# Where the projections' side work stands: stores a product later, pieces of x from the keys on, unpacking from the eighth product on

## The chip, the cores and the metric

The kernel runs on one core of a Trainium2 chip. The metric is the device time of one execution in microseconds (us), as the median of the runs; less is better. The engines are TensorE (PE), VectorE (DVE), ScalarE (ACT), GpSimd (POOL) and SyncE (SP), which here only issues DMAs. Each engine takes its instructions in the order of its own list.

## The reference, cut to what matters

One layer on x of 2 batches x 1024 tokens x 1024 columns. Both branches read the same layer norm.

```python
xn = _layernorm(x, axis=-1)
# attention: 32 heads of 32, 8 key/value heads, rotary angles on q and k, causal
q, k, v = xn @ wq, xn @ wk, xn @ wv          # 1024, 256 and 256 columns
s = softmax(mask(rope(q) @ rope(k).T / sqrt(32))) @ v @ wo
# feed-forward with 4-bit weights, 2 x 2752 columns inside
w_gu = scale[g_idx] * (nibble(qweight) - (nibble(qzeros) + 1)[g_idx])
gate, up = split(xn @ w_gu)
g = silu((silu(gate) * up) @ w_d)            # w_d is unpacked likewise
return x + s * g
```

## The kernel before

**Stages.** For each of the two batches the kernel makes the layer norm, turned so that the 1024 columns lie on partitions (`xnT`), then runs `project`, `attend` and `project_out`. The feed-forward of both batches comes last. `project` of batch 0 lies at about 27 to 258 us of the profile, that of batch 1 at about 700 to 912 us.

**Seven products for eight.** `project` multiplies `xnT` with five pairs of weight tiles, each tile 128 columns wide: pair 0 holds the first two tiles of the keys' weights, pairs 1 to 4 the queries'. (Keys have 256 columns, so one pair covers them.) A pair is done as a 2x2 block product in Strassen's manner: tokens, contraction and columns are halved, and sums of blocks (`sums` for x, `quarters` for weights) let seven products stand for eight. A product is four matmuls of 128x512 (eight PE instructions, 3.44 us at full clock, line L455). The generator `pair` yields after each, in the order 1, 5, 2, 6, 3, 7, 4. The loop over pairs interleaves two of these generators, so that product 4 of a pair comes after product 1 of the next: the variable `slot` numbers all products from 1 to 35, and slots 1 to 8 are products 1, 5, 2, 6, 3, 7 of the keys, 1 of the first pair of queries and 4 of the keys. After them `values(t)` makes the values `v` for eight blocks of 128 tokens (L503), with two buffers `ps_v` in PSUM that ACT copies out (L506).

**What a product sets off.** `sum_of` adds a product to an earlier sum (`u`, `p`: L466, L484, DVE); `turn_heads` applies the rotary angles (L417 and L419 on DVE, L420 and L421 on POOL) and puts a function `leave` on the list `leaving`. `leave` splits the rotated tile in a high part (`rot_hi`, ACT, L425) and the rest (`rot_lo`, DVE, L427), and issues both stores to DRAM on SP (L428, L429).

**Side work, in `others`.** `project` runs under `manual_schedule`: every engine gets its instructions in the order in which the program writes them. After each product `others(n)` is called:

```python
while len(leaving) > n:
    leaving.pop(0)()
if splits and slot % 2:
    splits.pop(0)()
next(side, None)
```

First come the splits of rotated tiles. Then, at odd slots, comes one piece of x (`split_x`): `x_hi` on ACT (L511), `x_lo` on DVE (L513) and two stores of 256 KB to `xs_dram` on SP (L514, L515); the feed-forward reads them later. There are 16 pieces in a batch, and four are put on the list with each pair from pair 1 on, so the first lies at slot 11, and the last two at slots 37 and 39, among the values. Last comes one step of `side`. In batch 0 that is `look`, which surveys the scales, zeros and group indices (L141 to L208 on DVE), reduces a flag to one number (`one`, L232, then a matmul at L234), and issues from ACT eight spreading loads `zb_gu` (L240) and 21 of `zb_d` (L245). In batch 1 it is `unpack` for eight units of 256 weight columns, 35 steps: SP loads `qw` and `zt` (L256, L258), DVE takes the nibbles (`nib`, L272 to L277), ACT makes floats (`nf`, L281), POOL issues the store to `ng` (L263).

**Loads and maxima.** In the loop over pairs, ahead of a pair's third product, SP is given the loads of the turned keys (`head.keys`, pair 1, L631), then of the values' weights (L370) and of the next pair's weights `w_qk` (L364); at pair 2 the 16 loads of turned queries (`head.queries`, L636). From there on `head.rows` makes the row maxima of the first head group's scores a step at a time between matmuls and among the values: products `s` on PE (L671, L677), maxima `mx` on DVE (L687), and `mrow` (L724). Two score buffers tie PE to the maxima.

**Pools.** `rot_hi`, `rot_lo`, `x_hi`, `x_lo`, `qw`, `zt` and `nib` have two buffers each.

Of the kernel before, what the change touches and what calls it, by code (L numbers as in the profile page):

```python
# [10 lines left out]
F32 = mybir.dt.float32  # L11
F32R = mybir.dt.float32r
# [6 lines left out]
ALU = mybir.AluOpType  # L19
# [4 lines left out]
P = 128  # L24
# [12 lines left out]
def block_kernel(  # L37
# [18 lines left out]
    nc = tc.nc  # L56
# [9 lines left out]
    NC = D // P  # L66
    KH = NS
    TB = 512
    NB = T // TB
# [44 lines left out]
    xs_dram = [dram.tile([2, P, NS, T], F32, name=f"xs_{b}", tag=f"xs_{b}") for b in range(B)]  # L114
# [251 lines left out]
    def load_kv(pool, w_dram, w=None):  # L366

        if w is None:
            w = pool.tile([P, NS, N_KV * HD], F32, name="w_kv")
        nc.sync.dma_start(w, w_dram.rearrange("(g p) n -> p g n", p=P))  # L370
        return w

    def project(b, xnT, w_k, qs, ks, v, side, head, S, places):
# [5 lines left out]
        with tc.tile_pool(name="qkv_w", bufs=1, reuse_waits="tile") as wp, tc.tile_pool(name="qkv", bufs=2, reuse_waits="tile") as pool, tc.tile_pool(  # L379
            name="qkv_t", bufs=1, reuse_waits="tile"  # L380
        ) as tp, tc.tile_pool(name="qkv_ps", bufs=3, space=PSUM, reuse_waits="tile") as psp, tc.tile_pool(
            name="v_ps", bufs=2, space=PSUM, reuse_waits="tile"
# [16 lines left out]
            def quarters(wa, wb):  # L399


                low, high = slice(0, H), slice(H, NS)
                t = [wp.tile([P, H, P], F32, name=f"t_{i}") for i in range(2)]
                nc.vector.tensor_tensor(t[0], wb[:, low], wa[:, low], ALU.subtract)
                nc.vector.tensor_tensor(t[1], wb[:, high], t[0], ALU.subtract)
                nc.gpsimd.tensor_tensor(wb[:, low], wb[:, high], wb[:, low], ALU.subtract)
                B = {1: wa[:, low], 2: wa[:, high], 3: wb[:, high], 5: t[0], 6: t[1], 7: wb[:, low]}
                yield B
                B[4] = wp.tile([P, H, P], F32, name="t_2")
                nc.gpsimd.tensor_tensor(B[4], wa[:, high], t[1], ALU.subtract)  # L410
                yield B

            def turn_heads(c, n, dst):

                tok = slice(n * TB, (n + 1) * TB)
                t1 = pool.tile([P, TB], F32, name="rot1")
                nc.vector.tensor_tensor(t1, c, cs[:, 0, tok], ALU.mult)  # L417
                t2 = pool.tile([P, TB], F32, name="rot2")
                nc.vector.stream_shuffle(t2, c, swap)  # L419
                nc.gpsimd.tensor_tensor(t2, t2, cs[:, 1, tok], ALU.mult)  # L420
                nc.gpsimd.tensor_tensor(t1, t1, t2, ALU.add)  # L421

                def leave():
                    hi = pool.tile([P, TB], F32R, name="rot_hi")
                    nc.scalar.copy(hi, t1)  # L425
                    lo = pool.tile([P, TB], F32R, name="rot_lo")
                    nc.vector.tensor_tensor(lo, t1, hi.bitcast(F32), ALU.subtract)  # L427
                    nc.sync.dma_start(dst[0, :, tok], hi.bitcast(F32))  # L428
                    nc.sync.dma_start(dst[1, :, tok], lo.bitcast(F32))  # L429

                leaving.append(leave)

            leaving, splits = [], []
            slot = 0

            def others(n=1):


                while len(leaving) > n:
                    leaving.pop(0)()  # L440
                if splits and slot % 2:
                    splits.pop(0)()
                next(side, None)

            def pair(B, dsts):

# [23 lines left out]
                product(1, A[0, 0], 0, True)  # L470
                nc.scalar.copy(p1, banks[0])
                others()
                yield
                product(5, S[0], 2, True)
                nc.scalar.copy(p5, banks[2])
                nc.gpsimd.tensor_tensor(p5, p1, p5, ALU.add)
                others(0)
                yield
                product(2, A[0, 1], 0, False)
                turn_heads(banks[0], 0, dsts[0])  # L480
                others()
                yield
                product(6, S[1], 1, True)
# [21 lines left out]
                    )  # L505
                nc.scalar.copy(v[:, t, :], ps)  # L506

            def split_x(c, n):
                tok = slice(n * TB, (n + 1) * TB)
                hi = xp.tile([P, TB], F32R, name="x_hi")  # L510
                nc.scalar.copy(hi, xnT[:, c, tok])  # L511
                lo = xp.tile([P, TB], F32R, name="x_lo")
                nc.vector.tensor_tensor(lo, xnT[:, c, tok], hi.bitcast(F32), ALU.subtract)  # L513
                nc.sync.dma_start(xs_dram[b][0, :, c, tok], hi.bitcast(F32))  # L514
                nc.sync.dma_start(xs_dram[b][1, :, c, tok], lo.bitcast(F32))  # L515

            def weights(i):
                return [load_w(places, wq, c, tag=f"room_{1 + NREP + c % 4}") for c in (2 * i - 2, 2 * i - 1)]  # L520
# [10 lines left out]
            for i in range(PAIRS):  # L531
                dsts = (ks[0], ks[1]) if i == 0 else (qs[2 * i - 2], qs[2 * i - 1])
                g = pair(B, dsts)
                next(g)
                for _ in running or ():
                    next(make)
                next(g)

                if i == 1:
                    head.keys()  # L540
                    w = load_kv(None, wv, w_k)
                if i == 2:
                    head.queries()
                if 0 < i < PAIRS - 1:
                    loads.append(weights(i + 1))
                if i:
                    splits += [lambda c=c, n=n: split_x(c, n) for c in (2 * i - 2, 2 * i - 1) for n in range(NB)]
                for _ in range(3):
                    next(g)
                if i == 2:  # L550

                    work = head.rows()
                if i + 1 < PAIRS:
                    make = quarters(*loads[i + 1])
                    B = next(make)
                next(g)
                running = g
            next(running)
            others(0)

            warm = tp.tile([P, 1], F32, name="warm")
            nc.scalar.activation(warm, eps, AF.Exp)
# [996 lines left out]
    def open_x():  # L1559
        st = ExitStack()  # L1560
        xp = st.enter_context(tc.tile_pool(name="x", bufs=1, side="right", reuse_waits="tile"))
        return st, xp.tile([P, NS, T], F32, name="xnT"), xp

    ffn_open = ExitStack()
    x_open, xnT, xp = open_x()
# [4 lines left out]
    for b in range(B):  # L1570
# [5 lines left out]
        with tc.tile_pool(name="at_first", bufs=1, reuse_waits="tile") as fp, tc.tile_pool(  # L1576
            name="qkv_T", bufs=1, reuse_waits="tile"
        ) as qp:

            room = [q0p.tile([P, T], F32R, name=f"room_{j}") for j in range(1 + NREP)]  # L1580
            v = qp.tile([P, NT, N_KV * HD], F32, name="v")
            with tc.tile_pool(name="ps_s", bufs=1, space=PSUM, reuse_waits="tile") as ps_s:
                head = Maxima(qs_dram[b], ks_dram[b], fp, ps_s, room)
                if b == 0:
                    with tc.tile_pool(name="prep", bufs=1) as pool, tc.tile_pool(
                        name="prep_ps", bufs=1, space=PSUM
                    ) as psp:
                        first = look(pool, psp)
                        project(b, xnT, w_k, qs_dram[b], ks_dram[b], v, first, head, oT, q0p)
                        for _ in first:  # L1590
                            pass
                else:
                    with tc.tile_pool(name="unpack", bufs=2, side="right", reuse_waits="tile") as up:
                        side = unpack(up, range(11, 19), False)
                        project(b, xnT, w_k, qs_dram[b], ks_dram[b], v, side, head, oT, q0p)
                        for _ in side:
                            pass
                x_open.close()

                room += [q0p.tile([P, T], F32R, name=f"room_{j}") for j in range(1 + NREP, 1 + 2 * NREP)]  # L1600
                output = Output(b, oT, q0p)
                attend(head, v, oT, output)
        if b == B - 1:
            ffn_args = start_ffn(ffn_open)
            xnT = xp = None
        else:
            x_open, xnT, xp = open_x()
        with tc.tile_pool(name="unpack", bufs=3, side="right", reuse_waits="tile") as up:
            side = unpack(up, range(11) if b == 0 else range(19, NF), b == B - 1)
# [62 lines left out]
```

## Time and profile before

| | |
|---|---|
| runs | 2365.11, 2359.92, 2359.94 us |
| median | 2359.94 us |
| profiled execution | 2352.96 us, span 2351.1 us, mean granted clock 0.983 |
| PE, DVE, ACT, POOL busy | 2222.8, 1528.2, 1142.2, 854.1 us |
| `project` of batch 0, about 231 us (27 to 258) | PE busy 180.09 us, DVE 140.28, ACT 32.10, POOL 80.13 |

The span runs from the first to the last instruction; 1.86 us of the profiled execution lie around it. A row of a timeline gives the start, the length, the engine (with q for its queue of DMA issues), the line, the operation, the tile written and the tiles read, a shape, a count, and in brackets the idle time ahead of it with what ended it. A row of waits gives who waited for whom, the total in us, how often, and the longest. A row of the table by stretch gives its ends and length, the busy time of PE, of PE's weight loads, of DVE, ACT and POOL with their instruction counts, then the granted clock of PE, the mean busy share of the DMA engines, and GB/s.

### The profile page before, as it was taken

To read this page: it belongs to the slowest core of one execution; us is meant where nothing else is said; L and a number is where in the kernel's file an instruction comes from. 1 tells how busy PE (TensorE), PEld (TensorE's weight loads), DVE (VectorE), ACT (ScalarE), POOL (GpSimd) and SP (SyncE) were. 2 spreads that over 40 slices of the span, in tenths; PEclk is the share of its full clock that TensorE was granted. 3 is DMA by queue.
4 is the path that set the end of the run, shared out by engine and by line. 5 is a ranking of instruction groups with operands and counts; after the bars stand their busy time and mean duration, and the time that the engine had idled before them with its cause. 6 is when DMAs were issued, how large, how long until landed. Compare 5 with 4: busy or idle time off the path is not lost.

```text
span 2351.1 us, 30837 instructions
## 1 busy us (share of the span) xinstructions
PE 2222.8 (95%) x11233; PEld 1530.0 (65%) x11233; DVE 1528.2 (65%) x2336; ACT 1142.2 (49%) x1838; POOL 854.1 (36%) x599
## 2 busy tenths in 40 slices
PE   7894999999998879999999999999999999999997
PEld 4343655554883446555547878888878888878875
DVE  7773477774436774777751366776778677777875
ACT  2111345544242223544451466555778655556875
POOL 3550376776035552777771200000135200000362
PEclk9997999999998999999999999999999999999999
DMA  5645131311476864322216923232555655332475
GB/s 156 212 156 189 39 88 46 82 46 31 158 229 209 250 206 104 88 49 60 67 34 230 314 69 81 57 78 81 222 173 196 197 139 144 94 81 94 131 232 154
DMA packets 262185, 309.52 MB, mean 132 GB/s; under 512 B 19147, under 2 KB 197707, under 8 KB 261880
## 3 DMA queue, kind: packets, MB, share of 16 engines
q1 hardware_dynamic: 245172, 260.62, 37.3%
q0 software_dynamic: 10752, 38.02, 5.3%
q10 hardware_dynamic: 6100, 8.82, 1.2%
q8 instruction: 91, 1.49, 0.3%
q14 instruction: 70, 0.57, 0.1%
HBM read 214.58 MB, written 97.03 MB: 133 GB/s over the span
## 4 chain that ended last, share of the span: by engine, by line
PE 73%; POOL 7%; DMA 6%; issue 6%; DVE 5%; ACT 2%; SPq 1%; ACTq 1%; POOLq 0%; DVEq 0%
PE acc L1321 27%; PE acc L1202 11%; PE st L784 7%; PE s L677 7%; PE o L831 5%; PE ps_wo L1003 5%; PE l L849 3%; PE ps_v L503 2%; PE st L799 2%; PE ps L455 2%; DMA w_qk<-in_L_attn_wq 1%; POOL rot L420 1%; PE s L671 1%; POOL rot L421 1%; POOL p L944 1%
## 5 line engine op out<-in xcount | busy, mean ns | idle before, releaser
L1321 PE MATMUL acc<-x,w 128*128 128x512 f32 x2752 | 640.3, 393 | 2.3 <-ACT acc L1089 1.3
L1321 PEld LDWEIGHTS acc<-x,w 128*128 128x128 f32 x2752 | 512.4, 188 | 121.7 <-DVE h L1294 7.4
L1091 DVE TENSOR_SCALAR acc<-acc,r_gu 128x1024 f32<-128x1024 f32 x301 | 389.1, 1293 | 166.0 <-PE acc L1321 162.5
L687 DVE TENSOR_REDUCE mx<-s 128x1 f32<-128x512 f32 (+3 forms) x672 | 383.9, 608 | 173.0 <-PE s L671 88.0
L809 ACT ACTIVATE p<-st 128x512 f32<-128x512 f32 (+3 forms) x768 | 314.7, 496 | 314.6 <-PE st L799 313.3
L1089 ACT ACTIVATE acc<-acc,r_gu 128x1024 f32<-128x1024 f32 x301 | 327.4, 1088 | 232.3 <-PE acc L1321 228.7
L1305 POOL TENSOR_TENSOR h_lo<-h,h_hi 128x512 fp32r<-128x512 f32 x78 | 100.3, 1287 | 805.4 <-PE acc L1202 588.9
L944 POOL TENSOR_TENSOR p<-p 128x2048 f32<-128x2048 f32 (+3 forms) x122 | 359.9, 2954 | 9.3 <-PE o L831 4.9
L1091 DVE TENSOR_SCALAR acc<-acc,r_d 128x512 f32<-128x512 f32 x320 | 241.6, 759 | 62.3 <-PE acc L1202 60.0
L1089 ACT ACTIVATE acc<-acc,r_d 128x512 f32<-128x512 f32 x320 | 210.9, 663 | 61.8 <-PE acc L1202 55.1
L1003 PE MATMUL ps_wo<-oT,w_o 128*128 128x256 f32 x1024 | 232.1, 382 | 0.0
L1202 PE MATMUL acc<-h_lo,w 128*128 128x512 f32 (+1 forms) x576 | 228.9, 397 | 2.9 <-POOL h_lo L1305 2.6
L1202 PE MATMUL acc<-h_hi,w 128*128 128x512 f32 (+1 forms) x576 | 229.5, 399 | 0.7 <-ACT h_hi L1304 0.7
L1003 PEld LDWEIGHTS ps_wo<-oT,w_o 128*128 128x128 f32 x1024 | 191.1, 190 | 40.9 <-issue 16.7
L812 POOL TENSOR_SCALAR_AFFINE_SELECT p<-p 128x512 f32<-128x512 f32 x128 | 80.3, 634 | 242.2 <-ACT p L809 242.2
L831 PE MATMUL o<-p,v 128*32 128x512 f32 (+3 forms) x1536 | 162.9, 496 | 0.9 <-POOL p L812 0.9
L677 PE MATMUL s<-kst,room 128*128 128x512 f32 (+3 forms) x384 | 130.5, 379 | 0.0
L1202 PEld LDWEIGHTS acc<-h_lo,w 128*128 128x128 f32 (+1 forms) x576 | 108.4, 188 | 30.7 <-POOL h_lo L1305 5.1
L1202 PEld LDWEIGHTS acc<-h_hi,w 128*128 128x128 f32 (+1 forms) x576 | 108.3, 188 | 30.6 <-issue 3.0
L784 PE MATMUL st<-room,kst 128*128 128x512 f32 (+3 forms) x384 | 119.1, 371 | 3.2 <-ACT p L809 3.2
L281 ACT ACTIVATE nf<-nib 128x1024 fp32r<-128x1024 uint8 (+2 forms) x68 | 67.7, 1039 | 90.5 <-DVE nib L277 40.0
L677 PE MATMUL s<-room,room 128*128 128x512 f32 (+3 forms) x96 | 52.9, 578 | 61.5 <-DVE mx L687 46.4
(193 smaller groups left out, 2705.1 us busy)
## 6 DMA issues: line engine op xcount, KB each, us to landing
w<-ng SPq DMA_DIRECT2D x86, 512.0 KB
w<-nd SPq DMA_DIRECT2D x63, 512.0 KB
ng<-nf POOLq DMA_DIRECT2D x42, 512.0 KB, 7.6
room<-qs SPq DMA_DIRECT2D x160, 128.0 KB
x<-xs SPq DMA_DIRECT2D x32, 512.0 KB
qst<-qs SPq DMA_DIRECT2D x96, 128.0 KB
xt<-in_L_attn_x SPq DMA_DIRECT2D x16, 512.0 KB
w_qk<-in_L_attn_wq SPq DMA_DIRECT2D x16, 512.0 KB
```

Of the source, the lines that this page charges most:

```text
L677: nc.tensor.matmul(s[:, c * w : (c + 1) * w], q[j][:, qt * P : (qt + 1) * P], k[:, k0:k1], start=n == 1, stop=c == n - 1 and (n > 1 or not ...
L687: nc.vector.tensor_reduce(mx[:, at, js[0] : js[0] + n, k0 // TB], s[:, : w * n].rearrange("p (j t) -> p j t", j=n), AX.X, ALU.max)
L784: nc.tensor.matmul(s[:, q0:], kst[g][:, kt * P : (kt + 1) * P], stack[g][j][:, qlo + q0 : qlo + TB], start=True, stop=False,)
L809: nc.scalar.activation(p[:, j, q0:], st[j][:, q0:], AF.Exp, scale=1.0 / math.sqrt(HD))
L831: nc.tensor.matmul(o[HD * j : HD * (j + 1), q0:], v[:, kt, HD * g : HD * (g + 1)], p[:, j, q0:], start=(kt == 0), stop=last,)
L944: what(*args)
L1003: self.last = nc.tensor.matmul(ps[:, c * self.BLK : (c + 1) * self.BLK], self.ws[c0 + c][:, g, :], self.oT[:, g, t0 : t0 + self.BLK], star ...
L1089: nc.scalar.mul(a, a, r)
L1091: nc.vector.tensor_scalar(a, a, r, None, ALU.mult)
L1202: nc.tensor.matmul(acc[c], w[:k, c * P : (c + 1) * P], ht[:k, :], start=(f == 0 and t == 0), stop=(t == 1), skip_group_check=(f > 0),)
L1305: nc.gpsimd.tensor_tensor(at[1][:k, :], h[:k, f, tok], at[0][:k, :].bitcast(F32), ALU.subtract)
L1321: nc.tensor.matmul(a[:, n, :], w[i][:, g * P : (g + 1) * P], xs[t][:, g, n * TB : (n + 1) * TB], start=(g == 0 and t == 0), stop=(t == 1), ...
```

## The change

Three things are altered in `project`. Stores of `rot_hi`, `rot_lo`, `x_hi` and `x_lo` are put on a list `going`, and `send` issues them at the start of the next `others`, and also ahead of `head.keys` and `head.queries`. A piece of x is made at every even slot from 2 on, so that the 16 are made at slots 2 to 32. In batch 1 `side` takes no step at slots 1 to 7; its 35 steps begin at slot 8, and the last of them come among the values. In batch 0 `side` is stepped as before.

```diff
                     lo = pool.tile([P, TB], F32R, name="rot_lo")
                     nc.vector.tensor_tensor(lo, t1, hi.bitcast(F32), ALU.subtract)
-                    nc.sync.dma_start(dst[0, :, tok], hi.bitcast(F32))
-                    nc.sync.dma_start(dst[1, :, tok], lo.bitcast(F32))
+                    going.append((dst[0, :, tok], hi))
+                    going.append((dst[1, :, tok], lo))
 
                 leaving.append(leave)
 
-            leaving, splits = [], []
+            def send():
+
+                for to, what in going:
+                    nc.sync.dma_start(to, what.bitcast(F32))
+                going.clear()
+
+            leaving, going = [], []
             slot = 0
 
             def others(n=1):
 
 
+                send()
                 while len(leaving) > n:
                     leaving.pop(0)()
-                if splits and slot % 2:
-                    splits.pop(0)()
-                next(side, None)
+                if slot % 2 == 0:
+                    next(splits, None)
+                if b == 0 or slot > 7:
+                    next(side, None)
...
-            def split_x(c, n):
-                tok = slice(n * TB, (n + 1) * TB)
-                hi = xp.tile([P, TB], F32R, name="x_hi")
-                nc.scalar.copy(hi, xnT[:, c, tok])
-                lo = xp.tile([P, TB], F32R, name="x_lo")
-                nc.vector.tensor_tensor(lo, xnT[:, c, tok], hi.bitcast(F32), ALU.subtract)
-                nc.sync.dma_start(xs_dram[b][0, :, c, tok], hi.bitcast(F32))
-                nc.sync.dma_start(xs_dram[b][1, :, c, tok], lo.bitcast(F32))
+            def split_x():
+                for c in range(NC):
+                    for n in range(NB):
+                        tok = slice(n * TB, (n + 1) * TB)
+                        hi = xp.tile([P, TB], F32R, name="x_hi")
+                        nc.scalar.copy(hi, xnT[:, c, tok])
+                        lo = xp.tile([P, TB], F32R, name="x_lo")
+                        nc.vector.tensor_tensor(lo, xnT[:, c, tok], hi.bitcast(F32), ALU.subtract)
+                        going.append((xs_dram[b][0, :, c, tok], hi))
+                        going.append((xs_dram[b][1, :, c, tok], lo))
+                        yield
+
+            splits = split_x()
...
+                send()
                 if i == 1:
                     head.keys()
                     w = load_kv(None, wv, w_k)
                 if i == 2:
                     head.queries()
                 if 0 < i < PAIRS - 1:
                     loads.append(weights(i + 1))
-                if i:
-                    splits += [lambda c=c, n=n: split_x(c, n) for c in (2 * i - 2, 2 * i - 1) for n in range(NB)]
...
             next(running)
             others(0)
+            send()
+            for _ in splits:
+                send()
```

## The prediction

> **What bounds the kernel now.** I read the page's sections on busy time and on the chain first, to see whose time counts.
>
> ```profile
> PE 2222.8 (95%) x11233; PEld 1530.0 (65%) x11233; DVE 1528.2 (65%) x2336; ACT 1142.2 (49%) x1838; POOL 854.1 (36%) x599
> PE 73%; POOL 7%; DMA 6%; issue 6%; DVE 5%; ACT 2%; SPq 1%; ACTq 1%; POOLq 0%; DVEq 0%
> ```
>
> PE is busy for 95%, and the change adds and removes no matmul. So it can act only through PE's waits inside the two `project` stages, and through the half clock that follows a long wait. The second view is therefore the list of PE's waits, over 25 to 262 us (batch 0) and then over 695 to 915 us (batch 1).
>
> ```profile
> PE s L677 <- DVE mx L687: 32.3, 4, 21.4
> PE ps L455 <- DVE u L484: 5.4, 1, 5.4
> PE ps_bad L234 <- DVE one L232: 1.8, 1, 1.8
> ```
>
> ```profile
> PE s L677 <- DVE mx L687: 14.1, 7, 7.6
> PE s L677 <- DMA room<-qs: 6.7, 4, 2.1
> PE ps L455 <- DMA w_qk<-in_L_attn_wq: 6.2, 1, 6.2
> PE ps L455 <- DVE u L484: 3.8, 1, 3.8
> ```
>
> Third, the timelines around the longest wait of each list: first ACT and SP in batch 0's values stage, then the row of that stage's last 18 us in the table by stretch.
>
> ```profile
> 207.26 0.37 ACT L506 COPY v<-ps_v 128x256 f32<-128x256 f32 x1 [6.28 <-PE ps_v L503]
> 207.32 24.77 ACTq L240 DMA_DIRECT2D zb_gu<-z_gu  x8
> 232.14 0.37 ACT L506 COPY v<-ps_v 128x256 f32<-128x256 f32 x1 [24.50 <-DMA room<-qs]
> 232.41 0.62 ACT L511 CAST x_hi<-xnT 128x512 fp32r<-128x512 f32 x1
> 233.23 15.40 ACTq L245 DMA_DIRECT2D zb_d<-z_d  x21
> ```
>
> ```profile
> 201.00 0.32 SPq L514 DMA_DIRECT2D xs<-x_hi  x1
> ...
> 202.17 1.97 SPq L631 DMA_DIRECT2D kst<-ks  x4
> 204.24 12.35 SPq L636 DMA_DIRECT2D qst<-qs  x16
> ```
>
> ```profile
> 217.00:235.00 18.00, 0.59 (x1) 0.50 (x2) 1.89 (x3) 0.89 (x2) 0.00 (x0) 0.50 0.95 283
> ```
>
> ACT spends 24.77 us issuing eight loads, and only then copies `v`, then makes the last `x_hi`. `x_lo` waits for that, the maxima `mx` stand behind `x_lo` on DVE, and PE waits 21.4 us for them. Meanwhile the DMA engines are 0.95 busy, and PE's clock ends at 0.50. SP had stood 16.1 us at the store of 201.00, from 184.8 on.
>
> Last, single rows where the pieces are to go:
>
> ```profile
> 67.48 1.75 DVE L427 TENSOR_TENSOR rot_lo<-rot,rot_hi 128x512 fp32r<-128x512 f32 x1
> 75.39 0.68 DVE L427 TENSOR_TENSOR rot_lo<-rot,rot_hi 128x512 fp32r<-128x512 f32 x1
> 718.85 0.53 DVE L272 TENSOR_SCALAR nib<-qw 128x512 uint16<-128x512 uint16 x1 [8.98 <-DMA qw<-in_L_ffn_qweight_gu]
> 758.79 6.71 PE L455 MATMUL ps<-xnT,w_qk 128*128 128x512 f32 x8 [6.17 <-DMA w_qk<-in_L_attn_wq]
> ```
>
> The same subtraction takes 0.68 us alone, and 1.75 us where POOL is in L476 (67.41 to 68.69); `x_lo` has its shape (0.67 to 1.76 us). In batch 1 DVE stood 8.98 us before the first unpacking, with PE's `u` behind it.
>
> **The change, batch 0.** Counts stay (16 pieces a batch, two stores each); only places move. Negative is faster.
>
> *Keys.* Five pieces (after products 2, 4, 6, 8 and 10) now lie on DVE ahead of the `u` of 74.79, which released PE after 5.43 us. DVE is busy without a gap from 45.77 to there. Two pieces fall into idle time before that (2.16, 0.52 and 0.71 us); three add 0.60 each beyond, 1.67 each beside POOL: +1.8 to +5.0, none below zero since nothing leaves this stretch. I take +2.2, near the lone row, as POOL is busy only 21.6 of the 53 us. The same delay comes to the key loads (70.30) and `w_qk` (72.64), which feeds the next product; it runs side by side, so only +0.3 (0 to 1) more.
>
> The Trainium skill, "SBUF — State Buffer", section "SBUF: two separate sides", says that a DVE operation with two SBUF inputs and a GpSimd operation that reads SBUF shut each other out for a whole instruction. The trace agrees: 1.75 against 0.68. Taken at its strictest it makes the keys' term +5.0, which rival D prices from the rows.
>
> *Queries.* SP's 16 loads (96.89, 8.11 us) made PE wait 2.04 and 2.30. A piece's two stores now stand between the last `qs` store and these: about 0.4 each to issue, 0.6 for `x_lo`, half a MB of traffic: 0.3 to 2.5, I take +1.3.
>
> *To the 35th product.* Eight pieces instead of eleven follow product 16: 0 to -1.8, I take -0.7, since PE seldom waits there. PE's wait of 8.71 at 187.11 stands behind POOL's rotation, `rot_lo`, `x_lo`, the prep's `inv` and `mx`: only 0.60 of it goes, -0.6.
>
> *Values.* Both pieces leave. `one` no longer waits behind `x_hi` and `x_lo`: of 1.78 some 0.45 stays, as in the tokens without a piece (0.37 to 0.55): -1.3. Between `v` (232.14) and the 21 issues `x_hi` goes: -0.8. The 21.4 us do not go: DVE and PE run on for one token, but the two buffers of `ps_v` then hold PE until ACT copies `v`, behind the same 24.77 us. What can shorten these is that SP, free of the 16.1 us stop, begins the key loads about 197 instead of 202, while the DMA is 0.25 busy. At 283 GB/s 5 us are 1.4 MB of the 8.6 MB (44 loads of 128 KB, eight of 344 KB) that must pass. But ACT's and SP's DMAs take turns on shared completion lanes, so not all of it counts: 0 to -6.0, I take -3.5.
>
> A page speaks against this term: the Trainium skill, "DMA: Bandwidth & Descriptors", section "Issuing engines are not separate DMA queues", says that DMAs from all issuing engines share the same 16 DMA engines. The 0.95 agrees. By it freeing an issuer moves nothing while they are full; only the earlier start counts, and at worst nothing (rival B).
>
> Sum: 2.2 + 0.3 + 1.3 - 0.7 - 0.6 - 1.3 - 0.8 - 3.5 = **-3.1**.
>
> **Batch 1.** *Keys.* Unpacking leaves products 1 to 7, so nothing holds DVE at 718.85 and PE's 3.79 goes, with 1.77 of slow clock (5.37 against 3.60). But POOL's memset of 718.24 waits for a store of the stage before and remains, with `p5` and the rotations behind it, so product 8 starts some 1.9 earlier, not 5.5. Then POOL's issue at 736.80 (1.73) goes and `nib` pairs (2.7) give way to pieces (0.7 to 1.75): the key loads and `w_qk` (issued 747.53, 12.0 us to land) come up to 3.7 earlier, and of the wait of 6.17 and the slow product behind it (6.71 against 3.60) part goes. Bounds -2 and -7; against it a first unpacking that waits for its load at product 9 (0 to 3). I take -4.5.
>
> *Queries:* one piece before SP's loads, as in batch 0, +1.3 (0.3 to 2.5); PE's four waits (6.7) show them exposed. *Later slots:* -0.7 (0 to -1.8). *Values:* the waits 1.65 and 1.86 stand behind `x_lo`, and 0.45 of each stays: -2.6; the one of 7.55 loses `x_lo`'s 0.60: together -3.2 (-2.5 to -4). In come seven unpacking steps: `nib` 0.28 and 0.43 on DVE, `nf` 1.05 on ACT: +1.0 (0 to 1.5), since they need no `v`.
>
> Sum: -4.5 + 1.3 - 0.7 - 3.2 + 1.0 = **-6.1**.
>
> Stores a product later cost nothing by themselves: tiles of `rot_hi` come round after three products or more, 10.3 us, and the store now leaves 3.4 of those later; what hides them is that 6.9 us remain.
>
> Together -9.2. The profiled execution of 2352.96 would become 2343.8. The median of the runs, 2359.94, lies 6.98 above that execution; the sum taken from it gives 2351.
>
> **Rivals.**
> A, the forecast: 2351, own range 2345 to 2353.
> B, the stages keep their ends: ACT's issues still end at 232 because the DMA is full (its -3.5 becomes 0), and `w_qk` of batch 1 lands as late as before (-4.5 becomes -2). -9.2 + 3.5 + 2.5 = -3.2: 2357. For it: 0.95 DMA, and POOL's memset.
> C, both open up: SP's early start counts fully (-6.0), `w_qk` is no longer waited for (-7.0), queries cost 0.3 twice, keys 1.8. -9.2 - 2.5 - 2.5 - 2.0 - 0.4 = -16.6: 2343. For it: the DMA's idle 0.75 before 200.
> D, slower: the full DVE of batch 0's keys makes `w_qk` late. All pieces meet POOL at 1.67 (+5.0 on `rot_lo`, `u` and the loads behind it); five pieces' 2.5 MB of stores stretch `w_qk` from some 9 us to batch 1's 12.0 (+3.0); PE, waiting over 3 us more, runs that product slowly (+3.1); queries +2.5. Less 0.7, 0.6, 1.3 and 0.8: +10.2; batch 1 at its worst keys and queries (-2 + 2.5 - 0.7 - 3.2 + 1.5 = -1.9). +8.3: 2368. It decides once `u` ends later than some 78 us instead of 75.5. Against it: POOL idles over half of this stretch.
>
> **How the numbers follow.** 0.3% is 7.1 us, about what a measurement of this kernel can tell from no change. A 0.45, B 0.25, C 0.13, D 0.17. Faster: C and most of A, 0.53; same: B and the rest of A, 0.30; slower: D, 0.17. The range leaves out the far half of D and of C: 2339 (C with half of its unknowns beyond) to 2366.
>
> **What would show it.** Right: no `x_lo` between `v` and `mx` in the values stages; PE's 21.4 replaced by waits for ACT's `v`; the eight issues ending before 232 less some 5; `u` at 77 and PE's wait for it at 7 to 8 in batch 0; no wait for `u` at 722 and a `w_qk` wait of 3 to 5 in batch 1. Wrong: `u` after 78, or a `w_qk` wait above 3 in batch 0 (D); an attention that waits for the last `ng` store, which now leaves near 895 and whose tile is wanted near 916.

## The result, and the profile after

The changed kernel took 2350.64 us in the median of four runs (2345.38 to 2351.71), against 2359.93 of the kernel before beside it: a ratio of 0.9953, 95% interval 0.9931 to 0.9975. A second set of runs (twelve, beside 23 of before) gave 0.9967, interval 0.9956 to 0.9978. So the change is worth some 8 us, and both intervals exclude no change. The forecast was 2351.

In the changed file the matmul of the products is L463 (before L455), `p` and `u` are L474 and L492 (L466, L484), the matmul of the values L511 and its copy L514 (L503, L506), `x_lo` L523 (L513), the key and query loads L646 and L651 (L631, L636), `mx` L702 (L687). From the page, the line of busy times and that of the chain:

```profile
PE 2224.7 (95%) x11233; PEld 1529.6 (65%) x11233; DVE 1528.4 (65%) x2336; ACT 1141.6 (49%) x1838; POOL 853.7 (36%) x599
PE 77%; POOL 7%; issue 5%; DVE 5%; DMA 3%; ACT 2%; SPq 1%; ACTq 0%; POOLq 0%; DVEq 0%
```

The counts are the same; DMA's share of the chain falls from 6% to 3%. PE's waits over 25 to 262 us, in the first fence, and over 690 to 915 us, in the second:

```profile
PE ps_v L511 <- ACT v L514: 23.6, 2, 12.6
PE s L692 <- DVE mx L702: 10.0, 4, 7.7
PE ps L463 <- DVE u L492: 7.4, 1, 7.4
```

```profile
PE s L692 <- DVE mx L702: 9.8, 7, 6.5
PE ps L463 <- DVE p L474: 9.6, 4, 5.4
PE s L692 <- DMA room<-qs: 7.3, 3, 4.6
PE ps L463 <- DMA w_qk<-in_L_attn_wq: 0.9, 1, 0.9
```

In batch 0 the 21.4 us behind `mx` have become 23.6 behind ACT's copy of `v`: another name for nearly the same time. The wait for `u` grew from 5.4 to 7.4. In batch 1 the wait for `w_qk` is gone (6.2 to 0.9), and that for `u` (3.8) has given way to one of 5.4 for `p`.

The timelines of ACT and SP in batch 0's values, and the row of the table by stretch:

```profile
209.42 23.65 ACTq L240 DMA_DIRECT2D zb_gu<-z_gu  x8
233.11 0.37 ACT L514 COPY v<-ps_v 128x256 f32<-128x256 f32 x1 [23.38 <-DMA zb_gu<-z_gu]
235.08 14.70 ACTq L245 DMA_DIRECT2D zb_d<-z_d  x21
```

```profile
201.40 2.09 SPq L646 DMA_DIRECT2D kst<-ks  x4
203.58 14.93 SPq L651 DMA_DIRECT2D qst<-qs  x16
```

```profile
217.00:235.00 18.00, 5.01 (x21) 3.88 (x21) 3.57 (x11) 0.37 (x1) 0.00 (x0) 0.68 0.95 283
```

The eight issues still take 23.65 us (24.77 before), at the same 0.95 and 283 GB/s. SP no longer stands 16.1 us at a store of `x_hi`, yet its key loads start at 201.40, only 0.77 earlier than before. Now they wait for the flag's `one`, which DVE makes at 201.19, as the list of SP's own waits shows:

```profile
SPq L646 <- DVE one L232: 13.9, 1, 13.9
```

In all fourteen profiles of this record these loads start 0.06 to 2.0 us after the end of `one`; before, it ended at 201.77 and the loads started at 202.17.

To see where the time went, I take from the trace the start of each product (the first of its eight PE instructions) and of the values. Mean lengths in us, of two profiles each (before: that of the start and e1; changed: that above and e5):

| stretch | before | changed | difference |
|---|---|---|---|
| batch 0, products 1 to 14 | 52.9 | 56.5 | +3.6 |
| 14 to 22 (queries) | 35.7 | 37.4 | +1.7 |
| 22 to the values | 70.7 | 68.8 | -1.9 |
| values | 71.0 | 68.5 | -2.4 |
| batch 1, products 1 to 15 | 63.8 | 58.1 | -5.8 |
| 15 to 22 (queries) | 35.1 | 36.0 | +0.8 |
| 22 to 35 | 59.7 | 63.1 | +3.3 |
| 35 to the end of the values | 53.1 | 50.9 | -2.2 |

(Differences are taken before rounding.) Batch 0 comes out at +1.0 and batch 1 at -3.8. Taking in further profiles in which a batch's program is the same (e4 for batch 0 of before; e6 for batch 0, and e9, whose batch 0 differs only in where three short memsets stand; e8, e10 and e11 for batch 1 of the changed kernel), batch 0 is 231.5 us before and 230.2 after, batch 1 211.8 and 207.5: -1.3 and -4.3. Between the batches nothing changes (442.5 and 442.3). These -5.6 lie within what the second ratio allows (-5.2 to -10.4 of 2358 us). Only batch 1's part is clear of the differences between profiles: its two lengths before are 210.7 and 212.8 us, its five after 206.7 to 208.6. Batch 0's -1.3 is less than the 4.3 us by which its three profiles of before differ.

### The profile page after: what moved, and what is told of

The parts are those of the page before. It is cut to its first block, busy times and chain, and to the rows that moved or that the text cites. A ratio compares the mean times of both kernels' runs of the same rounds, so it can differ in the third digit from the quotient of the medians.

```text
span 2348.0 us, 30834 instructions
## 1 busy us (share of the span) xinstructions
PE 2224.7 (95%) x11233; PEld 1529.6 (65%) x11233; DVE 1528.4 (65%) x2336; ACT 1141.6 (49%) x1838; POOL 853.7 (36%) x599
## 4 chain that ended last, share of the span: by engine, by line
PE 77%; POOL 7%; issue 5%; DVE 5%; DMA 3%; ACT 2%; SPq 1%; ACTq 0%; POOLq 0%; DVEq 0%
PE acc L1336 27%; PE acc L1217 11%; PE ps_wo L1018 10%; PE st L799 7%; PE s L692 7%; PE o L846 5%; PE l L864 3%; PE ps_v L511 2%; PE st L814 2%; POOL rot L420 2%; POOL rot L421 1%; DMA w_qk<-in_L_attn_wq 1%; PE s L686 1%; POOL p L959 1%; PE ps L463 1%
## 5 line engine op out<-in xcount | busy, mean ns | idle before, releaser
L702 DVE TENSOR_REDUCE mx<-s 128x1 f32<-128x512 f32 (+3 forms) x672 | 383.5, 608 | 186.7 <-PE s L686 91.4
L1217 PEld LDWEIGHTS acc<-h_lo,w 128*128 128x128 f32 (+1 forms) x576 | 108.4, 188 | 30.7 <-POOL h_lo L1320 5.2
L425 ACT CAST rot_hi<-rot 128x512 fp32r<-128x512 f32 x40 | 24.7, 617 | 189.1 <-POOL rot L421 178.8
L692 PEld LDWEIGHTS s<-kst,room 128*128 128x128 f32 x384 | 68.6, 188 | 61.1 <-DVE mx L702 31.6
```

What stands on the lines that cost most here:

```text
L692: nc.tensor.matmul(s[:, c * w : (c + 1) * w], q[j][:, qt * P : (qt + 1) * P], k[:, k0:k1], start=n == 1, stop=c == n - 1 and (n > 1 or not ...
L702: nc.vector.tensor_reduce(mx[:, at, js[0] : js[0] + n, k0 // TB], s[:, : w * n].rearrange("p (j t) -> p j t", j=n), AX.X, ALU.max)
L1217: nc.tensor.matmul(acc[c], w[:k, c * P : (c + 1) * P], ht[:k, :], start=(f == 0 and t == 0), stop=(t == 1), skip_group_check=(f > 0),)
```

## The experiments

All times are medians beside runs of the kernel before. e1 to e4 share one set of these, e5 to e8 another, e9 to e12 a third, so e9 to e12 are compared with the changed kernel only by way of the kernel before.

**e1, the kernel before again.** No edit.

> The kernel before, unchanged, to see how its executions differ among themselves: the profiled one took 2352.96 us, the others 2357.8 to 2365.1. If that execution was merely at the low end, a second profile lies near 2360, and its extra 7 us lie in a stretch that the change touches (the values of batch 0 or the two waits for w_qk) or in one that it does not touch (project_out, the feed-forward). In the first case the gain of the change differs between executions; in the second the two profiles, 3.1 us apart, understate it for a reason that has nothing to do with it. I expect a time ratio of 1.000 within 0.002.

2356.12 us, ratio 1.000 (0.9989 to 1.0012); its executions reach from 2352.29 to 2365.08. The second profile took 2353.37 and not 2360, so it does not show where the longer executions lose their time. It differs from the first by +1.5 in batch 0 and +2.1 in batch 1. In batch 0 the ends of the values lie at 257.96, 259.41 and (e4, the same program there) 261.99. So this stage by itself differs by 4 us between executions, and a single profile of it does not price the change.

**e2, only the stores a product later.** Stores go on `going`; `send` stands in `others` and ahead of the key and query loads. Of the diff, the stores of the rotated tiles; those of `x_hi` and `x_lo` change likewise:

```diff
-                    nc.sync.dma_start(dst[0, :, tok], hi.bitcast(F32))
-                    nc.sync.dma_start(dst[1, :, tok], lo.bitcast(F32))
+                    going.append((dst[0, :, tok], hi))
+                    going.append((dst[1, :, tok], lo))
```

> Only the stores leave a product later; pieces and unpacking stay where they were. Theory (the prediction's): it is worth nothing by itself, 0 within 3 us, at most -0.8 where SP no longer stands in front of the split in the values. Rival: SP's standing in front of each store was what held its loads, and the whole gain of 9 comes with this part: -6 to -9.

2358.71, ratio 1.0008 (0.9998 to 1.0017): nothing that can be told from no change. The rival, that this part carries the gain, falls.

**e3, only the pieces earlier.**

```diff
-                if splits and slot % 2:
+                if splits and slot % 2 == 0:
                     splits.pop(0)()
...
+            splits += [lambda c=c, n=n: split_x(c, n) for c in range(NC) for n in range(NB)]
```

(The line that filled `splits` pair by pair is gone.)

> Only the pieces of x move (even slots from 2); stores go at once, unpacking starts at the first product. Theory: batch 0 pays some +4 to +6 by the end of the 22nd product (u and w_qk late, queries), and gets it back among the values, where its end comes out 0 to +2 later; batch 1 gets back 3 among its values: 0 to -4 in all. Unpacking and pieces now share the first products of batch 1, so product 6 there starts no earlier than before (722.7). Rival: the pieces out of the values carry the whole gain, -7 to -10.

2353.23, ratio 0.9988 (0.9979 to 0.9998), some -3 us: the theory's size. Product 22 of batch 0 starts 92.2 after product 1 (before 87.8 and 89.5), and the values take 69.2 (70.3 and 71.7). Product 6 of batch 1 starts at 723.6, as late as before.

**e4, only the unpacking from the eighth product.**

```diff
-                next(side, None)
+                if b == 0 or slot > 7:
+                    next(side, None)
```

> Only unpacking begins at the eighth product of batch 1. Theory: product 6 of batch 1 starts at 719.5 and no longer at 722.8, product 14 some 4 us earlier against the stage's start, and among the values the last unpacking steps cost 1 to 3 in front of the two pieces that stay there: -2 to -5 in all. Batch 0 is as before within 0.5. Rival: POOL's memset holds the eighth product anyway, and nothing comes of it: 0 to +2.

2363.98, ratio 1.0041 (1.0027 to 1.0055): by the ratio 10 us slower. Half of the theory held: product 15 of batch 1 starts 55.3 after product 1, against 64.8 and 62.8 before. Then it is lost again, products 28 to 35 taking 42.6 against 33.9 and 35.6. PE's waits over 824 to 866 us, of e4 and then of e1:

```profile
PE ps L456 <- DVE p L467: 3.9, 1, 3.9
PE s L678 <- DVE mrow L725: 3.3, 1, 3.3
PE m_ps L723 <- DVE mt L712: 2.8, 1, 2.8
```

```profile
PE ps L455 <- DVE p L466: 2.3, 2, 1.2
PE s L677 <- DVE mrow L724: 2.1, 1, 2.1
PE m_ps L722 <- DVE mt L711: 1.6, 1, 1.6
```

DVE's list in e4, just before `mrow`:

```profile
836.51 1.76 DVE L514 TENSOR_TENSOR x_lo<-xnT,x_hi 128x512 fp32r<-128x512 f32 x1
838.19 1.35 DVE L272 TENSOR_SCALAR nib<-qw 128x512 uint16<-128x512 uint16 x1
839.57 1.37 DVE L277 TENSOR_TENSOR nib<-nib,zt 128x512 uint16<-128x512 uint16 x1
840.86 0.41 DVE L725 COPY mrow<-m_ps 128x512 bf16<-128x512 bf16 x1
```

A piece and an unpacking step, 4.5 us together, stand ahead of the `mrow` that PE waits for. In e1 only the piece does:

```profile
838.81 1.75 DVE L513 TENSOR_TENSOR x_lo<-xnT,x_hi 128x512 fp32r<-128x512 f32 x1
840.49 0.41 DVE L724 COPY mrow<-m_ps 128x512 bf16<-128x512 bf16 x1
```

Of the 7.0 us by which products 28 to 35 are longer in e4 than in e1, 4.0 are these three waits; in the rest PE is busy for longer, at a granted clock of 0.88 against 0.95. So the parts do not add: +2, -3 and +10 by the ratios, but -8 together. No two of the parts were run without the third, so which of them need each other is not shown. From this I took a new theory, that pieces and `nib` must stand at products of different parity, and tried it twice.

**e5, the changed kernel again.**

> The changed kernel once more, beside the same runs of the kernel before as the three below: 0.9955 of the time of before, about -10 us. The profiled execution was 3.1 us under that of before, the medians 9.3; the runs of before differ by 14 us, so the true gain may be less: -6 to -11.

2350.16, ratio 0.9967 (0.9956 to 0.9978), its executions 2345.56 to 2358.58: within what was expected.

**e6, the changed kernel with unpacking from the ninth product.** `slot > 7` becomes `slot > 8`, so that pieces and `nib` meet at even products.

> The changed kernel, with unpacking from the ninth product on in place of the eighth, nothing else. Theory: nib stands in every second step of unpacking, so an odd shift (7 products) puts it at odd products and a shift of 8 at even ones, where the pieces are; x_lo and nib then stand together on DVE in front of one product's sums and maxima, and PE's waits for p and mrow in products 20 to 35 of batch 1 grow by 4 to 7 us in all against the changed kernel: about as fast as before, 0.998 to 1.001 of it. Rival: only how early unpacking begins counts; then one product later is worth -0.5 to +1 against the changed kernel.

2348.34, ratio 0.9963 (0.9948 to 0.9977), the same as e5. Products 22 to 35 of batch 1 take 60.3, less than the changed kernel's 61.9 and 64.2. So it is not parity, and one product later makes no difference to the whole. But the run shows what an unpacking step ahead of `mrow` costs. DVE in the changed kernel, and then in e6:

```profile
836.11 1.36 DVE L272 TENSOR_SCALAR nib<-qw 128x512 uint16<-128x512 uint16 x1
837.50 1.44 DVE L277 TENSOR_TENSOR nib<-nib,zt 128x512 uint16<-128x512 uint16 x1
838.86 0.41 DVE L739 COPY mrow<-m_ps 128x512 bf16<-128x512 bf16 x1
```

```profile
834.55 0.67 DVE L427 TENSOR_TENSOR rot_lo<-rot,rot_hi 128x512 fp32r<-128x512 f32 x1
835.14 0.42 DVE L739 COPY mrow<-m_ps 128x512 bf16<-128x512 bf16 x1
```

Without the step PE waits 0.4 us for `mrow` (1.5 in the changed kernel, 3.2 in e5), and products 28 to 35 take 33.9 us (36.8 and 38.4; before 33.9 and 35.6). Part of this is given back around them: products 22 to 28 take 26.3 (25.0 and 25.9), and 35 to the end 51.8 (50.9 and 50.8).

**e7, e4 with the pieces at even products.** `slot % 2` becomes `slot % 2 == 0`.

> The kernel before, with unpacking from the eighth product on (as in e4) and pieces at even products instead of odd ones, from slot 10 on, so none among the keys; three instead of two pieces fall among the values. Theory: e4 lost because pieces and nib met at odd products; apart from each other, products 28 to 35 of batch 1 take 36 us instead of e4's 42.6, and the whole is 5 to 8 us under e4: 0.998 to 1.001 of before. Rival: e4 lost because unpacking was crowded into fewer products and into the values; then this is as slow as e4, 1.003 to 1.005.

2367.18, ratio 1.0038 (1.0024 to 1.0052), as slow as e4: the rival's number. Products 28 to 35 of batch 1 do come down, to 38.2. But a piece now stands behind the third token's `v`, and ACT meets it between the issues of batch 0:

```profile
209.22 0.59 ACTq L240 DMA_DIRECT2D zb_gu<-z_gu  x1
209.34 0.62 ACT L512 CAST x_hi<-xnT 128x512 fp32r<-128x512 f32 x1
213.18 23.95 ACTq L240 DMA_DIRECT2D zb_gu<-z_gu  x7
...
239.10 16.24 ACTq L245 DMA_DIRECT2D zb_d<-z_d  x21
255.38 0.37 ACT L507 COPY v<-ps_v 128x256 f32<-128x256 f32 x1 [17.85 <-DMA zb_d<-z_d]
255.65 0.62 ACT L512 CAST x_hi<-xnT 128x512 fp32r<-128x512 f32 x1
```

Another `x_hi` stands behind both blocks of issues, with `x_lo` and `mx` behind it: PE waits 36.8 us for `mx`, and the values take 81.5 us (70.3 and 71.7 before). This is the strongest sign that a piece behind ACT's issues is dear. As a test of parity it is spoiled by that.

**e8, batch 0's pieces at products 15 to 30, one each.**

```diff
-                if slot % 2 == 0:
+                if slot > 14 if b == 0 else slot % 2 == 0:
                     next(splits, None)
```

> The changed kernel, with the pieces of batch 0 at every product from 15 to 30 in place of every second from 2 to 32; batch 1 as changed. Theory: the keys' price in batch 0 goes (product 14 at 81 instead of 85.0, product 22 at 116 to 118 instead of 122.1), and the values start 3 earlier; their end, which ACT's issues set, comes 2 to 4 earlier: -2 to -4 against the changed kernel. Rival: a piece at every product crowds DVE beside the row maxima (DVE is busy for 52.8 of the 66 us from 112 to 178), and the 4 us come back as waits for mx and p: 0 to +2.

2357.32, ratio 1.0000 (0.9989 to 1.0011): the whole gain is lost, 7 to 8 us against e5, and the rival was right, at a higher price than I gave it. The keys' price does go: product 14 starts 54.0 after product 1 (56.5 in the changed kernel). But products 28 to 35 take 35.9 in place of 30.7. DVE in that stretch:

```profile
151.79 3.43 DVE L523 TENSOR_TENSOR x_lo<-xnT,x_hi 128x512 fp32r<-128x512 f32 x2
...
159.36 1.75 DVE L523 TENSOR_TENSOR x_lo<-xnT,x_hi 128x512 fp32r<-128x512 f32 x1
161.04 0.41 DVE L739 COPY mrow<-m_ps 128x512 bf16<-128x512 bf16 x1
```

Three pieces at 1.7 us each: two ahead of the reductions that make `mt`, one ahead of `mrow`, for which PE waits 2.1 us (0.4 in the changed kernel's batch 0). It is the same place as in e4.

**e9, the memsets of the maxima later.**

```diff
-            for mt in self.mts:
-                nc.gpsimd.memset(mt, 0.0)
...
         def rows(self):
+            for mt in self.mts:
+                nc.gpsimd.memset(mt, 0.0)
+            nc.gpsimd.memset(self.mxs[0][:, :, :, 1], MASKED)
```

> The changed kernel; the three POOL memsets of the maxima (mt twice, mx) stand at the start of head.rows, before product 21, and no longer ahead of product 1. Theory: in batch 1 the memset of 720.17, which waits for the store of sT, holds p5 and the rotations behind it on POOL, and so product 8 (5.36 us of waiting and 1.77 of slow clock). Without it product 8 of batch 1 starts 5 us earlier, product 15 some 3 to 6 earlier: -2 to -6 against the changed kernel. Rival: the load of w_qk, which the key stores set, or unpacking's first load, catches PE a few products later: 0 to -1.

2341.90, ratio 0.9935 (0.9923 to 0.9948): the lowest median of all, 7 to 8 us under the changed kernel. Its interval does not meet that of e5, but it overlaps that of the changed kernel's first four runs. POOL and PE at the start of batch 1 in the changed kernel, and then PE in e9:

```profile
720.17 0.98 POOL L635 MEMSET mt<- 128x512 bf16 x2 [9.95 <-DMA sT<-wo_r]
```

```profile
722.97 3.60 PE L463 MATMUL ps<-xnT,w_qk 128*128 128x512 f32 x8
731.93 5.37 PE L463 MATMUL ps<-xnT,t 128*128 128x512 f32 x8 [5.36 <-DVE p L474]
```

```profile
721.14 3.60 PE L463 MATMUL ps<-xnT,w_qk 128*128 128x512 f32 x8
724.57 3.60 PE L463 MATMUL ps<-xnT,t 128*128 128x512 f32 x8
```

Product 8 follows product 7 without a gap and at full clock. Of the 7.6 us gained by product 9, 7.1 are there at the end of the stage (200.1 us against 207.3). Nothing else in the stage took the wait's place.

**e10, the second survey of batch 0 eight products later.**

```diff
-        for part in parts[:2]:
-            yield from part
+        yield from parts[0]
+        for _ in range(NT):
+            yield
+        yield from parts[1]
```

(The idle steps behind these lines are eight fewer, so that the survey's number of steps stays.)

> The changed kernel; in batch 0 the second survey's four steps (some 12 us of DVE) stand 8 products later, the number of steps in all unchanged. Theory: in the keys of batch 0 DVE's list is full, and each us put into it ahead of u is a us for PE. Without these steps PE's wait of 7.4 for u is below 2, products 13 and 14 start 5 to 9 us earlier, and the end of batch 0's values moves by 2 to 6: -2 to -6 against the changed kernel. Rival: the steps only move to products 16 to 24, where DVE is as full beside the maxima and the rotations, and the gain is given back by product 28: 0 within 2.

2348.51, ratio 0.9964 (0.9952 to 0.9975), the same as the changed kernel: the rival's number. The wait for `u` falls from 7.4 to 1.4, which shows that DVE's list ahead of `u` set it, but the next product then waits 4.2 for `w_qk`. Product 14 starts 51.9 after product 1 instead of 56.5, and the values still start 3.7 earlier. Then the ACT issues take 25.47 and 16.34 us (23.65 and 14.70), and 2 us are left at the end.

**e11, six idle steps of the survey fewer.** `range(NC * NB + NT)` becomes `range(NC * NB + NT - 6)`.

> The changed kernel; six of the idle steps of the survey are left out, so that the flag is made and the 29 spreading loads are issued some six products earlier, before the values, where DMA is 0.2 to 0.45 busy. Theory: the end of batch 0's values is set by ACT's issues among them (PE waits 12.6 and 11.1 for v behind them), so PE's waits for v fall under 5 in all and the stage ends 8 to 15 earlier: -8 to -15. Rival: ACT, held by its issues between products 31 and 35, is late with rot_hi and the copies of p, and PE waits there instead: +5 to -3.

2355.70, ratio 0.9998 (0.9987 to 1.0009), 5 to 7 us slower than the changed kernel: the rival, at or above its upper end. ACT in e11, and PE:

```profile
175.96 26.68 ACTq L240 DMA_DIRECT2D zb_gu<-z_gu  x7
202.76 0.62 ACT L425 CAST rot_hi<-rot 128x512 fp32r<-128x512 f32 x1 [30.15 <-DMA room<-qs]
```

```profile
204.49 0.58 PE L692 MATMUL s<-room,room 128*128 128x256 f32 x1 [13.51 <-DVE mx L702]
225.12 0.80 PE L692 MATMUL s<-room,room 128*128 128x512 f32 x1 [17.58 <-DVE mx L702]
```

The issues are no quicker some 33 us earlier (the first is at 171.54, the row has the other seven), for SP's head loads move up with the flag, to 179.41, and run beside them again. ACT's `rot_hi` now stands behind them, `rot_lo` and `mx` behind that, and PE waits there instead.

**e12, e9, e10 and e11 together, with unpacking from the ninth product.**

> The changed kernel with all three: memsets at head.rows, second survey 8 products later and six idle steps fewer; and unpacking from the ninth product. If the three places are separate, their gains add: -12 to -22 against the changed kernel, 2330 to 2340. If they stand for one another (a stage's end is set by the DMA whatever comes before it), not more than the best of them alone.

2345.18, ratio 0.9957 (0.9942 to 0.9971): not better than e9 alone, and far from the sum. e9's gain in batch 1 is whole (199.1 us against 207.5), and its profile, the quickest of its executions, took 2338.43. e11's edit is in it, which cost 5 to 7 alone. e9 with e10 and without e11 was not run.

## Why the prediction was right, and which steps were not

The total and its direction came out: 2351 forecast, 2350.64 measured. Not every step did.

*Keys of batch 0*, +2.5 with `w_qk`: measured +3.6, inside the bounds. `u` was to run at 77 with a wait of 7 to 8; it ran at 77.64 with 7.4, and e10 confirms the cause. The term was small by 1: three of the five pieces ahead of it met POOL and took 1.75, only the first of these in idle time.

*Queries*, +1.3 each: +1.7 and +0.8. *Later slots and the 0.60*, -1.3 in batch 0: -1.9 up to the values; right.

*Values of batch 0*, -5.6: measured -2.4, or -3.8 with e4 and e6 taken in. The mis-sized term is the -3.5 for SP's earlier start. SP came off the stop of 16.1 us into another of 13.9: its loads wait for `one`, so they started at 201.4 and not at 197. What was argued about DVE and PE, that they run on for one token and then wait for `v`, is what the waits of 12.6 and 11.05 show. Here rival B had the right number for the term. Its reason, a full DMA, was not tested, since in no run did SP's loads start ahead of the flag. The Trainium skill, "DMA: Bandwidth & Descriptors", section "Issuing engines are not separate DMA queues", says that DMAs started by different engines run on the same 16 DMA engines, and so it also pointed this way. The trace agrees: the stretch is at 0.95 and 283 GB/s in both profiles. But ACT and SP also wait for each other's loads, as the prediction's taking of turns has it: SP's query loads stood 7.0 us for landings of ACT's `zb_gu`, and before, a landing of SP's `room` ended the wait of ACT's `v`. How much of the 23.65 us is the full DMA and how much these waits stays open.

*Keys of batch 1*, -4.5: -5.8 to product 15, right in size but not in its make-up. PE's wait of 3.8 for `u` went, yet product 8 started 30.3 and 29.2 us after product 1, where it had been 31.3 and 30.4: the memset alone held it, as e9 shows. I gave 1.9 for that and it was about 1. And the loads of `w_qk` were not issued earlier (46.8 after product 1, before 47.0). They landed earlier, as the chain of waits shows, of before and then of the changed kernel:

```profile
748.15 12.00 DMA w_qk<-in_L_attn_wq
```

```profile
749.07 7.96 DMA w_qk<-in_L_attn_wq
```

Before, POOL issued two `ng` stores of 512 KB each at 736.80 and again at 748.08, beside this load; afterwards it issues none between 709 and 764. That these stores were what stretched the load is supported by every profile: from its first issue to the start of product 14, which waits for it, pass 9.5 to 11.3 us in the four with stores beside it (before, e1, e2, e3) and 6.9 to 7.5 in the ten without. Before, SP also issued a `qw` load right behind it, at 750.46; e3 has the stores without that and stands at 9.5, so the stores are some 2 to 3 us of the 4.

*Products 22 to 35 of batch 1*, -0.7: measured +3.3, or +2.6 with e8, e10 and e11 taken in. This is the step that failed outright. I counted pieces and unpacking steps as small costs wherever PE seldom waits, and did not ask what stands ahead of `mt`, `mrow` and the last `p`, where PE always waits. e4 and e8 show that place dear, by their rows of DVE, and e6 by taking one unpacking step of 2.8 us away from `mrow`: products 28 to 35 became 3 to 4 us shorter, as short as before. e6 moves every unpacking step, so this is no clean price of one step. Why e4's other executions were up to 9 us slower than its profiled one stays open.

*Values of batch 1*, -3.2 + 1.0: -2.2. Right; the waits behind `x_lo` fell to 0.36 and 0.56.

*Stores later*, nothing: e2 says the same. *Rival D* did not come: `u` ended at 78.3, about at the point named, but `w_qk` was waited for only 0.43. The last `ng` store left at 893.1, and ACT went on with the attention without waiting for it.

So the direction came out and its causes in part, but that the total agrees to a microsecond is chance. By the stretches of the two pairs of profiles the change gave -2.8, by all profiles -5.6, where the sum said -9.2; the two failed terms were both too hopeful, by 2 to 3 and by 3 to 4, and only the keys of batch 1 gave 1 more than forecast. The medians gave -9.3 over four runs and -8.0 over twelve, with an interval that is 5 us wide even there. The 2359.94 from which the 2351 was counted moves as well: later sets of the kernel before have medians of 2355.48 to 2358.21. What the unprofiled executions of before lose beyond its two profiles could not be seen.

## What to carry to other kernels

Before you move side work in an ordered kernel, list the few places where the busiest engine always waits for the one that does this work, and look what the move puts ahead of them: with one unpacking step of 2.8 us ahead of `mrow`, seven products took 3 to 4 us more than without it. When a wait on one engine goes, look for the next engine that was waiting at the same time for something else; POOL's memsets of 1 us held batch 1 for 7 us, and moving them was worth about as much as the whole change. Parts of a change that only redistribute work do not add: measured singly these gave +2, -3 and +10 us, together -8.

## What the runs showed of the hardware that was not expected

The load of two weight tiles, issued by SP, took 12.0 us to land beside two `ng` stores of 512 KB each, issued by POOL, and a `qw` load, and 7.96 without either. With the stores and without the `qw` load (e3), the product that waits for it started 9.5 us after the first issue, against 11.3 and 6.9.

ACT's eight spreading loads took 24.8, 23.7 and 25.5 us to issue where they began at 207, 209 or 204 us (before, changed, e10), and in e11 the last seven took 26.7 from 176 us, SP's 44 head loads running beside them each time.
